# Expert results fetched ahead, three rounds apart, and three contexts moved behind the last expert tile, in a two-layer decoder

## The chip, the cores and the metric

The kernel runs on one core of a Trainium2 chip. The metric is the device time of one execution in microseconds (us). A core has five engines that matter here, each with its own list of instructions that it takes in order: PE (matrix products), DVE (elementwise work and reductions along rows), ACT (functions such as tanh, and copies out of PSUM), POOL (a second, general engine, which here does elementwise products, powers and the indirect transfers) and SP (which only issues transfers). Engines wait for each other by semaphores. On-chip memory is SBUF; matrix products land in PSUM, whose banks are handed round.

## The reference

The input is 32 sequences of 128 tokens with 256 channels. Six blocks follow one another, each added to its input:

```python
x = x + attn(layernorm(x))                 # layer 0: attention over a latent
x = x + xattn(layernorm(x), ctx)           # attention to a context, with distance bias
x = x + ffn(layernorm(x))                  # 2 of 8 experts for each token
x = x + mixer_mlp(x)                       # layer 1: gated linear recurrence, then an MLP
x = x + xattn1(layernorm(x), ctx)          # language-vision attention
x = x + ffn1(layernorm(x))                 # quantised MLP with a convolution over 3 tokens
```

The expert block and the recurrence are what the change touches the neighbourhood of:

```python
weights, top_idx, mask = router(x, Wr, br, top_k=2)
for e in range(8):
    h = relu(x @ W1[e] + b1[e])
    out += (h @ W2[e] + b2[e]) * weights[:, :, e] * mask[:, :, e]

u = k * v                                  # per chunk of 64 tokens
prefix = cumprod(a); acc = cumsum(u / max(prefix, 1e-6))
states = prefix * (state + acc)
y = gate * (q * states) + (1 - gate) * v
```

## The kernel before, in words

The kernel has three phases. `attention()` (until about 655 us) does layer 0's two attentions and the routing weights. `phase_c()` (until about 1221 us) sorts the tokens by expert and runs the experts. `layer1()` does all of layer 1.

**Experts.** Tokens are handled in tiles of 256 tokens of one expert. `brought` loads a tile's weights and gathers its tokens by an indirect transfer on POOL (L807), `tokens` turns them on PE and copies them out (L820), `first_layer` makes h (L832), `second_layer` makes y and adds the bias on DVE (L844), and SP writes the result to the tensor `ys` in HBM (L845). 36 tiles are always needed (`some`); `rest` holds up to a few more, each inside `tc.If(tiles > j)` (L862), where `tiles` is a register that every engine holds. Each engine has a branch at this place.

**Contexts.** Layer 1's language-vision attention needs keys and values of the context, for 16 units of two sequences (T = 256 tokens). `context(u, …)` (L659) returns three pieces: `load` (SP brings the turned context, L666), `keys` (8 matmuls `ck`, then two ACT evictions, L677) and `values` (8 matmuls `cv`, a DVE add, L686, and a write of both to the tensor `ckv` by SP, L690). The first `CTX0 = 6` units are done in `phase_c()` ahead of the expert tiles (L789 to L794), each wholly before the next. The other ten are laid into layer 1's rounds by `CTX_ROUNDS` (L926): for each unit the rounds of its load, keys and values.

**Layer 1.** `unit(u)` (L1043) returns the pieces of one unit of two sequences, 16 units in all. Their order is written by hand: `PLAN` (L910) lists rounds and the names of pieces, and the loop at L1394 walks over rounds t; in a round, it first emits the context pieces filed in `between`, and then, for each unit u, the pieces that PLAN has for round t − STEP·u, with STEP = 11. So a new unit begins every 11 rounds, a unit lasts 90 rounds, and up to nine units are in the air. The instructions of each engine stand in the order in which they are emitted, except that a scheduler may place some POOL instructions; `tc.keep_in_program_order` pins those it is given.

The pieces that the steps below speak of:

- `gather` (L1049): one indirect transfer on POOL (L1054) fetches 128 rows of `ys`, a token's result of one of its two experts, into a tile `yr`, of which there are five buffers. Two sequences times two experts make four per unit. It is pinned in program order.
- `added` (L1060): four DVE instructions (L1063) that add the weighted `yr` to x.
- `d_stats` to `d_flip`: moments on DVE (L967, L968), the inverse root on POOL (`rs_d`, L975; a second one is `rs_d2i` and so on), normalised rows on ACT (L986, L993), the flip on PE (`pt_d`) and its copy `hT_d` on ACT (L1005).
- `d_q`, `d_a`, `d_k`, `d_g`, `d_v`: five products on PE with evictions on ACT; `d_v` also has the product `u_d` on POOL (L1113).
- `d_scan1` (L1136 to L1141), `d_scan2` (L1144, L1145): the recurrence as two scans on DVE; `al_d` is its small copy at L1141. `d_rms` has the product `qn_d` on POOL (L1123).
- `d_state`: a product on DVE (L1148) and a difference `pre_d` on POOL (L1149), which is pinned too. `d_gate` (L1152, L1154) makes `yT_d`.
- `m_y` (L1159) and `m_stats`: x_m on DVE, its inverse root `rs_m` and the sum into x (L1169) on POOL; then the MLP `m_fc`, `m_out`.
- `e_stats`, `e_k`, `e_s`, `e_at` …: the language-vision attention, with the inverse root `rs_e` on POOL.
- `f_h`, `f_z`, `f_taps`, `f_silu`, `f_top` …: the quantised MLP in four quarters; `f_taps` has `z_f` on DVE (L1314) and POOL (L1320), `f_silu` is on ACT (L1327), `f_top` finds the largest absolute values on DVE (`top_f`, L1333).

At layer 1's start, SP loads `we` (L942) and `wc` (L1382), POOL clears the tile `first` (L946), and then the contexts' loads (`cT_k`) and the first fetches follow.

Of the kernel before, what the change touches and what calls it, by code (L numbers as in the profile page):

```python
# [75 lines left out]
def decoder(ctx: ExitStack, tc: tile.TileContext, a: dict, out: bass.AP):  # L76
# [13 lines left out]
    def bank(name, dt=F32):  # L90
        return psp.tile([P, 512 if dt == F32 else 1024], dt, tag="ps", name=name)
# [38 lines left out]
    def vec(name):  # L130
        at, w = PV[name]
        return pv[:, at : at + w]

    def row(name):
        at, w = RV[name]
        return rv[:, at : at + w]
# [68 lines left out]
    def mm(out, lhsT, rhs, start, stop):  # L205
        tc.keep_in_program_order(PE.matmul(out, lhsT=lhsT, rhs=rhs, start=start, stop=stop))  # L206
# [17 lines left out]
    NU = NB // U  # L224
# [434 lines left out]
    def context(u, wcs, turned_tile, kv_tile):  # L659

        wc = wcs.rearrange("p (w c m) -> p w c m", w=2, c=2)
        t = {}

        def load():
            t["cT"] = turned_tile(f"cT_k{u}")
            nc.sync.dma_start(  # L666
                out=t["cT"], in_=a["ctxT"][:, u * T : (u + 1) * T].rearrange("(c p) t -> p c t", p=P)
            )

        def keys():  # L670
            t["kv"] = kv_tile(f"kvc_{u}")
            p = bank(f"ck_{u}").rearrange("p (c t) -> p c t", c=2)
            for c in range(2):
                for k in range(2):
                    mm(p[:, c, :], wc[:, 0, k, c * P : (c + 1) * P], t["cT"][:, k, :], k == 0, k == 1)
            for c in range(2):
                A.activation(  # L677
                    t["kv"][:, 0, c * T : (c + 1) * T], p[:, c, :], AF.Identity, bias=vec("b_lk")[:, c : c + 1]
                )

        def values():
            p = bank(f"cv_{u}").rearrange("p (i d) -> p i d", i=U)
            for i in range(U):
                for c in range(2):
                    mm(p[:, i, :], t["cT"][:, c, i * S : (i + 1) * S], wc[:, 1, c, :], c == 0, c == 1)
            V.tensor_tensor(  # L686
                t["kv"][:, 1].rearrange("p (i d) -> p i d", i=U), p,
                row("b_lv")[:, None, :].to_broadcast([P, U, D]), ALU.add,
            )
            nc.sync.dma_start(out=ckv[u], in_=t["kv"])  # L690

        return load, keys, values

    def load_d():
        w = wpool.tile([P, D_W], F32, tag="w1", name="wd")
        for k in range(2):
            h = D_W // 2
            nc.sync.dma_start(out=w[:, k * h : (k + 1) * h], in_=a["wd"][:, k * h : (k + 1) * h])
        return w


    def phase_c():
        with tc.tile_pool(name="pc", bufs=2) as pool, tc.tile_pool(name="pc1", bufs=1) as keep:
# [82 lines left out]
            V.tensor_scalar(who, pk[:, :NJ], float(NTOK // 2), None, ALU.add)  # L786
            V.tensor_copy(slots, sl)

            for u in range(CTX0):  # L789
                for piece in context(  # L790
                    u, wcs, lambda n: pool.tile([P, 2, T], F32, tag="cT", name=n, bufs=4),
                    lambda n: pool.tile([P, 2, U * D], F32, tag="kv", name=n, bufs=4),
                ):
                    piece()  # L794
            wf = keep.tile([P, 4096], F32, name="wf")

            def brought(j):
# [15 lines left out]
            def tokens(t):  # L813
                j, w, xr = t
                xT = pool.tile([P, 2, TS], F32, tag="xTs", name=f"xTs_{j}")
                pt = bank(f"xs_{j}")
                for h in range(TS // P):
                    for c in range(2):
                        turned(pt[:, c * TS + h * P : c * TS + (h + 1) * P], xr[h][:, c * P : (c + 1) * P])
                V.tensor_copy(xT.rearrange("p c t -> p (c t)"), pt)  # L820
                return j, w, xT

            def first_layer(t):
                j, w, xT = t
                w1 = w[:, : 2 * FF].rearrange("p (c h) -> p c h", c=2)
                b1 = w[:, 2 * FF + NHC * D :]
                hT = pool.tile([P, NHC, TS], F32, tag="hTs", name=f"hTs_{j}")
                for hc in range(NHC):
                    p = bank(f"h_{j}_{hc}")
                    for c in range(2):  # L830
                        mm(p[:, :TS], w1[:, c, hc * P : (hc + 1) * P], xT[:, c, :], c == 0, c == 1)
                    A.activation(hT[:, hc, :], p[:, :TS], AF.Relu, bias=b1[:, hc : hc + 1])  # L832
                return j, w, hT

            def second_layer(t):
                j, w, hT = t
                w2 = w[:, 2 * FF : 2 * FF + NHC * D].rearrange("p (k d) -> p k d", k=NHC)
                b2 = w[:, 2 * FF + NHC * D + NHC :]
                yt = pool.tile([P, TS // P, D], F32, tag="yt", name=f"yt_{j}")
                for h in range(TS // P):  # L840
                    y = bank(f"y_{j}_{h}")
                    for hc in range(NHC):
                        mm(y[:, :D], hT[:, hc, h * P : (h + 1) * P], w2[:, hc, :], hc == 0, hc == NHC - 1)
                    V.tensor_tensor(yt[:, h, :], y[:, :D], b2, ALU.add)  # L844
                nc.sync.dma_start(  # L845
                    out=ys[j * TS : (j + 1) * TS, :].rearrange("(h p) d -> p h d", h=TS // P), in_=yt
                )
# [12 lines left out]
            def rest(j):  # L860
                if j < NT:
                    with tc.If(tiles > j):  # L862
                        second_layer(first_layer(tokens(brought(j))))
                        rest(j + 1)

            t = tokens(brought(0))
            for j in range(some):
                following = brought(j + 1) if j + 1 < some else None
                if j == 1:
                    wd = load_d()  # L870
                    nc.sync.dma_start(out=wf, in_=a["wf"])
                now = first_layer(t)
                t = tokens(following) if following else None
                second_layer(now)
                if j == 3:
                    ternary(wf, keep)
                    for c in range(2):
                        for part, v in (
                            (wd[:, c * 1280 : (c + 1) * 1280], "n1"),
                            (wd[:, 3072 + c * FF : 3072 + (c + 1) * FF], "n2"),  # L880
                        ):
                            A.activation(part, part, AF.Copy, scale=vec(v)[:, c : c + 1])
            rest(some)
        return wd

    def ternary(wf, keep):
# [21 lines left out]

    STEP = 11
    PLAN = (  # L910
        (0, "gather0 gather1"), (1, "gather2 gather3"), (3, "added"), (4, "d_stats"), (5, "d_nb"),
        (6, "d_norm"), (7, "d_scaled"), (8, "d_flip"), (10, "d_q d_a"), (11, "d_k d_g d_scan1"),
        (13, "d_v d_q2"), (14, "d_rms d_scan2"), (15, "d_state"), (16, "d_gate"), (18, "m_y"),
        (19, "m_stats"), (20, "m_scaled"), (22, "m_flip"), (26, "m_fc0 m_fc1"), (27, "m_fc2 m_fc3"),
        (29, "m_out0"), (30, "m_out1 m_out2"), (31, "m_out3"), (32, "e_stats"), (33, "e_nb"),
# [6 lines left out]
    )  # L922


    CTX0 = 6
    CTX_ROUNDS = (  # L926
        (0, 0, 0), (0, 1, 1), (0, 2, 2), (0, 3, 3), (1, 4, 5), (2, 6, 7), (4, 9, 9), (6, 12, 12),
        (9, 14, 15), (12, 16, 17),
    )

    def layer1(wd):
# [8 lines left out]
        with tc.tile_pool(name="pl", bufs=1) as pool, tc.tile_pool(name="pl1", bufs=1) as keep:  # L940
# [442 lines left out]
            between = {}  # L1383
            for u in range(CTX0, NU):
                for piece, r in zip(
                    context(
                        u, wcs, lambda n: sb("d", n, 4), lambda n: sb("kv", n, 2, shape=(2, U * D)),
                    ),
                    CTX_ROUNDS[u - CTX0],
                ):  # L1390
                    between.setdefault(r, []).append(piece)
            units = [unit(u) for u in range(NU)]
            pieces = {r: names.split() for r, names in PLAN}
            for t in range(STEP * (NU - 1) + PLAN[-1][0] + 1):  # L1394
                for piece in between.get(t, ()):
                    piece()
                for u in range(NU):
                    for name in pieces.get(t - STEP * u, ()):
                        units[u][name]()

    attention()
    wd = phase_c()
    routed.close()
    layer1(wd)


# [82 lines left out]
def program(arrays):  # L1489
    import concourse.bacc as bacc  # L1490

    nc = bacc.Bacc("TRN2", target_bir_lowering=False, num_devices=1)
    args = {
        k: nc.dram_tensor(f"in_{k}", v.shape, mybir.dt.from_np(v.dtype), kind="ExternalInput").ap()
        for k, v in arrays.items()
    }
    out = nc.dram_tensor("out", arrays["x"].shape, F32, kind="ExternalOutput").ap()
    with tile.TileContext(nc) as tc:
        decoder(tc, args, out)
    return nc  # L1500
# [9 lines left out]
```

## Time and profile before

| | us |
|---|---|
| median of 5 runs (lowest to highest) | 2036.15 (2033.29 to 2042.11) |
| profiled execution | 2037.04 |
| its span | 2035.3 |
| mean granted PE clock in it | 0.949 |
| busy: PE, DVE, ACT, POOL | 1823.2, 1168.7, 1082.7, 438.0 |
| last expert result written by DVE | 1221.2 |
| first fetch of an expert result, last one | 1224.7, 1827.6 |
| first product of layer 1's contexts | 1232.2 |

The span is the stretch from the first to the last instruction that the hardware profiler saw in one execution; the time of that execution lies a little above it. The granted clock is the share of full speed that PE was given.

In the lines of a profile, L1054 is line 1054 of the kernel. A line of the timeline has start, duration, engine, line, operation, output<-inputs, sizes, and in brackets how long the engine sat idle before it and what ended this. A line of the chain of waits has start, length, and the piece that the end of the kernel waited for at that time, followed back from the last instruction. A line of a group has the count, shortest, median and longest duration in ns, and the first and last start. A line of windows has the stretch, its length, and the busy time of PE, PE's weight loads, DVE, ACT and POOL in it, each with its count of instructions, then the granted clock, the busy share of the DMA engines and GB/s.

### The profile page before, as it was taken

The page shows a single profiled execution, that of the slowest core. Times are in us where ns is not written, and L with a number is a line of the kernel's source. Part 1 is how long each engine was busy: PE and PEld are TensorE (multiplying, and loading weights), DVE is VectorE, ACT ScalarE, POOL GpSimd, SP SyncE. Part 2 cuts the span into 40 slices and gives each one's busy share as a digit, 9 for nine tenths or more (in the row PEclk, how much of TensorE's full clock was granted, in tenths as well). Part 3 has the DMA queues.
Part 4 walks back from the last instruction along what each step waited for, and adds up shares of the span by engine and source line. Part 5 has one row for each costly group of instructions (what it writes and reads, how often), then busy time and mean ns, then how long its engine had stood idle before and what let it go on. Part 6 is the DMA issues. An engine that isn't in the chain of part 4 may idle for free.

```text
span 2035.3 us, 35569 instructions
## 1 busy us (share of the span) xinstructions
PE 1823.2 (90%) x13496; PEld 1496.3 (74%) x13496; DVE 1168.7 (57%) x3716; ACT 1082.7 (53%) x2600; POOL 438.0 (22%) x445
## 2 busy tenths in 40 slices
PE   6999999899987899999999997899998888899863
PEld 4777766677665688888888886678777777777752
DVE  6877667788777512111111013446788778888787
ACT  4454548878785522222222222455666666667662
POOL 4100000000000111111111102333444444443211
PEclk8999999989998799999999998999999999999976
DMA  4000010111002845555555535101011010010000
GB/s 156 3 2 3 7 38 22 33 32 53 12 22 70 293 169 197 183 212 173 210 182 202 196 120 181 52 21 32 22 32 32 27 37 27 27 37 21 27 11 21
DMA packets 53965, 162.65 MB, mean 80 GB/s; under 512 B 5664, under 2 KB 36512, under 8 KB 48672
## 3 DMA queue, kind: packets, MB, share of 16 engines
q1 hardware_dynamic: 47264, 142.52, 19.8%
q0 software_dynamic: 6528, 17.83, 3.1%
q8 instruction: 108, 1.77, 0.3%
q14 instruction: 65, 0.53, 0.1%
HBM read 133.33 MB, written 27.00 MB: 79 GB/s over the span
## 4 chain that ended last, share of the span: by engine, by line
PE 50%; DVE 25%; ACT 10%; POOL 7%; issue 4%; DMA 3%; SPq 0%; POOLq 0%; DVEq 0%; ACTq 0%
PE h L206 12%; PE y L206 12%; ACT sd_b L531 4%; PE od_a L206 3%; DVE top_f L1333 3%; DMA yr<-ys,slots 2%; DVE sd_b L518 2%; PE st_a L206 2%; POOL u_d L1113 1%; POOL z_f L1320 1%; DVE rd_a L497 1%; PE et_b L209 1%; PE ck L206 1%; DVE nm L444 1%; PE q_a L206 1%
## 5 line engine op out<-in xcount | busy, mean ns | idle before, releaser
L832 ACT ACTIVATE hTs<-h,moe 128x256 f32<-128x256 f32 x288 | 136.6, 474 | 374.2 <-PE h L206 374.2
L206 PE MATMUL h<-xTs,moe 128*128 128x256 f32 x1152 | 254.8, 379 | 2.6 <-DVE xTs L820 2.5
L206 PE MATMUL y<-moe,hTs 128*128 128x256 f32 x1152 | 254.6, 379 | 0.0
L206 PEld LDWEIGHTS h<-xTs,moe 128*128 128x128 f32 x1152 | 218.6, 190 | 32.8 <-DVE xTs L820 2.8
L206 PEld LDWEIGHTS y<-moe,hTs 128*128 128x128 f32 x1152 | 216.2, 190 | 27.9
L531 ACT ACTIVATE sd_b<-sd_b,nan_b 128x128 f32<-128x128 f32 x512 | 173.8, 388 | 28.6 <-DVE nan_b L525 28.4
L807 POOL DMA_INDIRECT xr<-xs,who x72 | 68.5, 951 | 437.2 <-PE xs L209 397.9
L820 DVE COPY xTs<-xs 128x512 f32<-128x512 f32 x36 | 24.9, 691 | 234.1 <-PE xs L209 234.1
L844 DVE TENSOR_TENSOR yt<-y,moe 128x256 f32<-128x256 f32 x72 | 30.6, 425 | 215.6 <-PE y L206 215.6
L206 PE MATMUL f_m<-hT_m,wd 128*128 128x256 f32 x512 | 121.1, 391 | 2.6 <-DVE x L1368 2.6
L206 PE MATMUL m_m<-wd,sT_m 128*128 128x256 f32 x512 | 119.8, 382 | 3.5 <-ACT sT_m L1180 3.4
L518 DVE CUSTOM_DVE_ANT_0 sd_b<-nd_b,s_b 128x128 f32<-128x128 f32 x512 | 113.1, 279 | 5.3 <-PE s_b L206 5.3
L206 PEld LDWEIGHTS f_m<-hT_m,wd 128*128 128x128 f32 x512 | 98.0, 197 | 18.0 <-DVE x L1368 4.6
L206 PEld LDWEIGHTS m_m<-wd,sT_m 128*128 128x128 f32 x512 | 95.4, 191 | 16.9 <-ACT sT_m L1180 4.8
L1320 POOL TENSOR_TENSOR z_f<-z_f,e_f 128x508 f32<-128x508 f32 x64 | 70.9, 1107 | 170.8 <-ACT e_f L1318 107.8
L1314 DVE SCALAR_TENSOR_TENSOR z_f<-d_f,pv,z_f 128x254 f32<-128x254 f32 x128 | 64.3, 507 | 58.7 <-ACT z_f L1304 58.3
L1327 ACT ACTIVATE z_f<-z_f 128x512 f32<-128x512 f32 x64 | 40.3, 630 | 104.1 <-POOL z_f L1320 104.0
L497 DVE RECIPROCAL rd_a<-od_a 128x256 f32<-128x256 f32 x32 | 56.0, 1751 | 63.0 <-PE od_a L206 63.0
L544 POOL COPY dens_b<-den_b 128x256 f32<-128x256 f32 x32 | 12.9, 402 | 363.0 <-DVE den_b L542 202.1
L474 ACT ACTIVATE et_a<-st_a 128x512 f32<-128x512 f32 x128 | 66.5, 613 | 27.6 <-PE st_a L206 27.6
L1304 ACT ACTIVATE z_f<-d_f,pv 128x256 f32<-128x256 f32 x128 | 69.6, 590 | 20.6 <-DVE d_f L1299 20.6
L444 DVE TENSOR_REDUCE nm<-s_a 128x4 f32<-128x512 f32 x128 | 79.0, 680 | 2.6 <-PE s_a L206 2.6
(358 smaller groups left out, 4067.8 us busy)
## 6 DMA issues: line engine op xcount, KB each, us to landing
moe<-in_moe SPq DMA_DIRECT2D x36, 2180.0 KB, 9.8
ys<-yt SPq DMA_DIRECT2D x36, 256.0 KB, 2.3
ckv<-kvc SPq DMA_DIRECT2D x16, 512.0 KB, 2.8
kv_e<-ckv SPq DMA_DIRECT2D x16, 512.0 KB, 3.5
x<-in_x SPq DMA_DIRECT2D x8, 512.0 KB, 9.0
cT_b<-in_ctxT SPq DMA_DIRECT2D x8, 512.0 KB, 6.0
xs<-xn_c SPq DMA_DIRECT2D x8, 512.0 KB, 3.0
cT_k<-in_ctxT SPq DMA_DIRECT2D x16, 256.0 KB, 4.7
```

The source lines that it names most:

```text
L206: tc.keep_in_program_order(PE.matmul(out, lhsT=lhsT, rhs=rhs, start=start, stop=stop))
L444: V.tensor_reduce(nms[i % 2][:, at : at + 2 * (P - HD)].rearrange("p (e x) -> p x e", e=2)[:, :2, :], sp[r], AX.X, ALU.max, negate=True,)
L474: A.activation(et[:, r].rearrange("p j q -> p (j q)"), st[r], AF.Exp)
L497: V.reciprocal(rd, od[:, 2 * S :])
L518: V.tensor_tensor_reduce(sd[:, r, j, :], nd[:, i, :], sp[r][:, j, :], SLOPES[head(r, j)], -3e38, ALU.add, ALU.max, mx[:, 4 * r + j : 4 * r ...
L531: A.activation(sd[:, r, j, :], sd[:, r, j, :], AF.Exp, bias=nan[:, 4 * r + j : 4 * r + j + 1], accum_out=den[:, h : h + 1] if r % 2 else None,
L807: GP.indirect_dma_start(out=xr[h], out_offset=None, in_=xs[:, :], in_offset=bass.IndirectOffsetOnAxis(ap=who[:, q : q + 1], axis=0),)
L832: A.activation(hT[:, hc, :], p[:, :TS], AF.Relu, bias=b1[:, hc : hc + 1])
L1304: A.activation(o["z"][:, hc, :], o["d", k][:, j, :], AF.Identity, scale=cw[:, hc, 1:2], bias=cb[:, hc : hc + 1],)
L1314: V.scalar_tensor_tensor(z[:, :, 1:], d[:, j, :].rearrange("p (b t) -> p b t", b=U)[:, :, : S - 1], cw[:, hc, 0:1], z[:, :, 1:], ALU.mult, ...
L1320: GP.tensor_tensor(z[:, :, : S - 1], z[:, :, : S - 1], e.rearrange("p h (b t) -> p (h b) t", b=U)[:, :, 1:], ALU.add,)
L1333: V.tensor_reduce(o["top"][:, k, :], o["z"][:, 4 * k : 4 * k + 4, :].rearrange("p h t -> p t h"), AX.X, ALU.max, apply_absolute_value=True,)
```

## The change

Two things are moved; no operation is added or taken away.

Contexts: those of units 0 to 5 are made as before. Those of units 6, 7 and 8, formerly in layer 1's rounds, are now loaded directly after them in `phase_c()`, and their keys and values stand behind the last of the 36 sure expert tiles, before `rest(some)` with its branches. Seven units, 9 to 15, are left to layer 1's rounds, with rounds of their own.

Fetches: `gather0` to `gather3` and `added` leave PLAN. They are filed in `between`, unit by unit three rounds apart: unit u has them in rounds 3u, 3u + 1 and 3u + 3 in place of 11u, 11u + 1 and 11u + 3, so the last is in round 48 in place of 168. In a round they stand behind the context pieces and ahead of PLAN's pieces of that round. The first piece of PLAN is now `d_stats` in round 4 of its unit. As `gather` and `d_state`'s difference on POOL are both pinned, POOL takes them in the order of the rounds.

```diff
+    CTX_FIRST, CTX0 = 6, 9
...
-            for u in range(CTX0):
-                for piece in context(
+            contexts = [
+                context(
                     u, wcs, lambda n: pool.tile([P, 2, T], F32, tag="cT", name=n, bufs=4),
                     lambda n: pool.tile([P, 2, U * D], F32, tag="kv", name=n, bufs=4),
-                ):
+                )
+                for u in range(CTX0)
+            ]
+            for pieces in contexts[:CTX_FIRST]:
+                for piece in pieces:
                     piece()
+            for pieces in contexts[CTX_FIRST:]:
+                pieces[0]()
...
+            for pieces in contexts[CTX_FIRST:]:
+                for piece in pieces[1:]:
+                    piece()
             rest(some)
...
     PLAN = (
-        (0, "gather0 gather1"), (1, "gather2 gather3"), (3, "added"), (4, "d_stats"), (5, "d_nb"),
-        (6, "d_norm"), (7, "d_scaled"), (8, "d_flip"), (10, "d_q d_a"), (11, "d_k d_g d_scan1"),
+        (4, "d_stats"), (5, "d_nb"), (6, "d_norm"), (7, "d_scaled"), (8, "d_flip"), (10, "d_q d_a"),
+        (11, "d_k d_g d_scan1"),
...
-    CTX0 = 6
+
+    FETCH = ((0, "gather0 gather1"), (1, "gather2 gather3"), (3, "added"))
+    FETCH_STEP = 3
+
     CTX_ROUNDS = (
-        (0, 0, 0), (0, 1, 1), (0, 2, 2), (0, 3, 3), (1, 4, 5), (2, 6, 7), (4, 9, 9), (6, 12, 12),
-        (9, 14, 15), (12, 16, 17),
+        (0, 3, 3), (0, 4, 4), (1, 5, 5), (2, 6, 6), (4, 7, 7), (6, 9, 9), (9, 12, 12),
     )
...
             pieces = {r: names.split() for r, names in PLAN}
+            for u in range(NU):
+                for r, names in FETCH:
+                    for name in names.split():
+                        between.setdefault(FETCH_STEP * u + r, []).append(units[u][name])
             for t in range(STEP * (NU - 1) + PLAN[-1][0] + 1):
```

## The prediction

> **What bounds the kernel now.** I read four views: the page, the chain of waits over one steady period of layer 1, the groups of the fetch, and the timelines of POOL and PE. The page first:
>
> ```profile
> PE 1823.2 (90%) x13496; PEld 1496.3 (74%) x13496; DVE 1168.7 (57%) x3716; ACT 1082.7 (53%) x2600; POOL 438.0 (22%) x445
> PE 50%; DVE 25%; ACT 10%; POOL 7%; issue 4%; DMA 3%; SPq 0%; POOLq 0%; DVEq 0%; ACTq 0%
> ```
>
> PE is busy 90% of the span, but only half of the chain runs through it: layer 1 (from 1222 us on) is a loop through DVE, ACT and POOL in which PE has little slack. One period, in the chain of waits, with pieces left out:
>
> ```profile
> 1779.06 0.84 POOL rs_e L975
> 1779.92 2.87 DMA yr<-ys,slots
> 1782.81 0.48 DVE x L1063
> ...
> 1788.93 1.81 DVE top_f L1333
> ...
> 1792.90 3.50 POOL u_d L1113
> ```
>
> The fetch of an expert result (yr) stands directly behind rs_e. DVE waits 2.87 us for it, does the first of four adds (L1063), and top_f and u_d come after. The same three lines start the next period at 1822.81, so a period is 43.75 us. The group of the fetch:
>
> ```profile
> L1054 POOL DMA_INDIRECT yr<-ys,slots x64: 945/984/1923, 1224.7 to 1827.6; - x64
>   DVE x L1063: 31.2, 34
> DMA to landing us min/median/max: 2.7/3.3/6.2
> ```
>
> All 64 adds together waited 31.2 us for these transfers. Last, the timeline of POOL at six of the sixteen u_d, with the start of layer 1 ahead of them:
>
> ```profile
> 1222.71 0.53 POOL L946 MEMSET first<- 128x512 f32 x1 [63.19 <-SPq L862]
> 1224.73 0.95 POOL L1054 DMA_INDIRECT yr<-ys,slots  x1 [1.50 <-issue]
> 1271.61 1.27 POOL L1113 TENSOR_TENSOR u_d<-u_d,v_d 128x512 f32<-128x512 f32 x1 [22.36 <-ACT v_d L1111]
> 1299.91 1.27 POOL L1113 TENSOR_TENSOR u_d<-u_d,v_d 128x512 f32<-128x512 f32 x1 [1.97 <-ACT v_d L1111]
> 1335.05 1.27 POOL L1113 TENSOR_TENSOR u_d<-u_d,v_d 128x512 f32<-128x512 f32 x1 [0.36 <-ACT v_d L1111]
> 1367.27 1.26 POOL L1113 TENSOR_TENSOR u_d<-u_d,v_d 128x512 f32<-128x512 f32 x1
> 1836.89 3.49 POOL L1113 TENSOR_TENSOR u_d<-u_d,v_d 128x512 f32<-128x512 f32 x1 [6.27 <-ACT v_d L1111]
> 1877.72 2.89 POOL L1113 TENSOR_TENSOR u_d<-u_d,v_d 128x512 f32<-128x512 f32 x1 [8.26 <-ACT v_d L1111]
> ```
>
> The first units follow each other in 28.3, 35.1 and 32.2 us, the last two in 40.83. No fetch lies between those last two (the final one starts at 1827.6), while intervals of u_d with fetches take 43.8. PE at the seam and in the loop:
>
> ```profile
> 1232.21 2.04 PE L206 MATMUL ck<-cT_k,wc 128*128 128x256 f32 x4 [11.45 <-DMA yr<-ys,slots]
> ...
> 1818.69 3.31 PE L206 MATMUL q_d<-hT_d,wd 128*128 128x256 f32 x8 [2.15 <-ACT hT_d L1005]
> 1821.80 2.30 PE L206 MATMUL a_d<-hT_d,wd 128*128 128x256 f32 x8
> ```
>
> PE stands still 11.45 us between the experts and layer 1, and 2.15 us in a period before q_d.
>
> **The change, part by part.** The numbers of fetches (64), adds (64) and contexts (16) stay as they are. Everything is a matter of place.
>
> *Start of the expert stage.* Three keys/values pairs leave it, but the first copy of tokens was held by the contexts and by two long reductions on DVE. It now stands ahead of the reductions. Reading the order by hand, the first h comes some 1.5 us earlier: −1.5. The three loads still issued there put the load of wf behind two context buffers on SP, about 6 us later; tile 0's 14 us hide that.
>
> *The seam.* The three pairs (ck and cv 1.73 us each by issue spacing, 3 × 3.46 = 10.4 us) now follow the last y at 1220.76. They look as if they filled the gap of 11.45 us. But in each engine's list they stand ahead of the branch that closes the sure tiles, and POOL's memset of `first`, the load of `we`, `wc` and the four cT loads on SP and the fetches on POOL come behind it. At present `first` starts 1.50 us after DVE's last yt ends (1221.21). DVE's last new kvc ends near 1220.8 + 10.4 + 0.7 = 1232, so the first fetch moves from 1224.73 to about 1234.3, and layer 1's first ck from 1232.21 to about 1243: +10.5. The gap is moved behind the contexts. Five pairs stand ahead of unit 0's flip in place of six: −3.46. Against that, adds of units 1 and 2 stand between kvc groups on DVE, and q_d of unit 0 needs the bank that such a kvc frees: about +2. Net **+9**. Bounds: +5 if the adds hold nothing, +11 if they hold a whole pair; and below nothing, about −3.5, if the branch does not hold POOL and SP (a rival below).
>
> *The first units (u_d0 to u_d3).* Before, POOL issues 12 fetches in these 95.66 us; after, I count 44 there (20 come earlier, none later). A fetch costs 0.95 + 0.30 us to the next issue, so 32 more are 40 us of POOL. If all fell into POOL's idle time they would cost 0; if all stood on the chain, 40. The windows of this stretch show how much room there is:
>
> ```profile
> 1258.00:1300.00 42.00, 37.55 (x171) 31.15 (x170) 17.29 (x42) 19.14 (x37) 12.30 (x12) 1.00 0.31 111
> ```
>
> POOL (fifth sum) is idle 30 of 42 us, but it takes its list in order. In unit 0, eight fetches stand around pre_d (8 × 1.25 = 10 us), and the eight adds that they feed stand ahead of x_m on DVE; x_m moves from 11.7 us behind u_d0 to 18.7. Four more fetches stand ahead of rs_m, which moves from 16.3 to 25.6. Part of it is caught by slack ahead of u_d1, 28.3 → 34.2 (+5.9). From u_d1 to u_d2, eight fetches precede qn_d (10 us) and PE has that much less of unit 0's work: 35.1 → 39.4 (+4.3). From u_d2 to u_d3, sixteen fetches (20 us) are interleaved: 32.2 → 39.5 (+7.3). That is +17.5; work made ready meanwhile (v_d and its Ln) returns about 2.5 behind it. I take **+15** of the 40, nearer to nothing because most of POOL's row is idle; bounds +8 (two units' delays absorbed) to +25. yr has five buffers; at one fetch in 1.25 us and 2.7 to 3.3 us to land, four are in flight, so buffers bind only where an add is late.
>
> [...] The gather's cost beside DVE first: the copy al_d (L1141) has 155/961/1761 ns as shortest, median and longest, the long ones beside a gather that itself takes 1.69 instead of 0.95. [...] The clock: in 1818 to 1822 the granted clock is 0.65 after a PE wait of 2.15 us, and q_d and a_d spread over 5.25 us between issues instead of 3.46. [...]
>
> *The steady part.* From u_d4 on there are no fetches or adds. From the chain, 2.87 of DMA and four adds of 0.4 to 0.5 leave, and al_d falls from 1.68 (its piece of the same chain) to about 0.16. That is not all gained: z_f of the last quarter (POOL 1.10, then ACT silu) ends only a little earlier and takes their place, so that top_f and u_d come 0.94 us sooner in the half behind rs_e. In the other half, hn_d leaves ACT's queue ahead of e_f0, and z_f, rs_m and hT_d come about 1.9 sooner. Together **2.8 per period**. The row of the last interval, 43.8 − 40.83 = 2.97, says nearly the same without my ordering. Bounds: 0.94 (only the first half) to 4.4 (43.7 − 39.3, PE's own list in a fetch-free stretch, waits for hT_d and at_e removed). Eight full periods (u_d6 to u_d14): 8 × 2.8 = 22.4. Three shorter ones ahead (37.35, 42.6 and 38.6 now): 3 + 4 + 1 = 8, estimated from the fetch's wait and the four adds that leave each. The last period and the 157.6 us behind u_d15 hold no fetch: 0. Sum **−30.4**, bounds −14 to −43.
>
> **Sum.** 2035.3 − 1.5 + 9 + 15 − 30.4 = 2027.4 of span. The profiled run took 2037.04 with a span of 2035.3; the median of the runs, 2036.15, lies 0.85 above that span, so **2028**.
>
> **The rivals.** *POOL's in-order list becomes the bound of the first units* (slower). Its place is rs_m, rs_d and u_d behind fetches between u_d0 and u_d3. For: 44 fetches in a stretch whose chain crosses POOL four times a unit. Against: 30 of 42 us idle. Price: 22 of the 32 additional fetches on the chain, +28, the seam +11, the steady part −20: 2035.3 − 1.5 + 11 + 28 − 20 + 0.85 = 2053.7, about 2053. It decides from where seam and ramp together exceed 38 us. *z_f's last quarter takes the fetch's place* in each period (slower): gain 8 × 0.94 + 8 = 15.5, 2042. For: silu is the next input of top_f. Against: the interval of 40.83. *PE's list is all that is left* (faster): 8 × 4.4 + 8 = 43 with ramp +10: 2010. For: h_f and at_e wait no more in the fetch-free stretch. Against: DVE is 35.66 of 43.76 us busy, and u_d still waits for ACT. *The contexts do fill the gap*, as they would if POOL and SP ran past the branch: seam near 0, 2018. For: 11.45 idle on PE against 10.4 of work. Against: `first` shows 63.19 us idle behind SP's branch before it.
>
> **How the numbers follow.** 0.3% (6.1 us) is about what a measurement can tell from no change. Forecast (own range 2014 to 2041) 0.40: of it 0.22 faster, 0.12 within, 0.06 slower, as 2028 lies only 2 us beyond the bound of 2030. POOL's list 0.22, slower. z_f's place 0.14: 0.10 slower, 0.04 within. PE's list 0.13 and the filled gap 0.11, both faster. Faster 0.46, same 0.16, slower 0.38. The range reaches to PE's list with a shorter ramp (2004) and just beyond POOL's list (2055).
>
> **What would show it.** Seam: the first fetch near 1234 and the first layer-1 ck near 1243, with PE idle about 11 us between; near 1225 and 1232, the rival holds. Ramp: u_d0 near 1280 and u_d3 near 1393 (1367.27 now), POOL nearly full of L1054. Steady: rs_e to rs_e near 41 us from unit 6 on, no yr in the chain, q_d waiting less than 2.15, al_d 0.16 long. I am wrong if u_d0 to u_d3 takes over 125 us, or under 100, or if the period stays above 42.5.

## The result, and the profile after

The changed kernel takes 2040.95 us (median of 30 runs, 2034.37 to 2044.13) where the kernel before takes 2035.82 (57 runs). The ratio is 1.0022, with a 95% interval of 1.0016 to 1.0027: slower, by less than the 0.3% that the prediction set as its limit for no change. The forecast was 2028 us, a gain. The profiled execution has a span of 2038.2 us, 2.9 above that of before.

Cut into stretches by the last expert result on DVE and by POOL's u_d of single units, the two profiled executions compare as follows. Each row is a difference of two starts in the timelines.

| stretch (us) | before | after | difference | forecast |
|---|---|---|---|---|
| start to last expert result | 1220.8 | 1217.9 | −2.9 | −1.5 |
| last expert result to u_d0 (the seam) | 50.8 | 67.9 | +17.0 | +9 |
| u_d0 to u_d3 (the first units) | 95.7 | 123.1 | +27.5 | +17.5 |
| u_d3 to u_d6 | 118.6 | 116.6 | −2.0 | −10.5 |
| u_d6 to u_d14 (eight periods) | 351.0 | 317.8 | −33.2 | −22.4 |
| u_d14 to u_d15 | 40.8 | 38.9 | −1.9 | 0 |
| u_d15 to the end | 157.6 | 156.0 | −1.6 | 0 |
| sum | 2035.3 | 2038.2 | +2.9 | −7.9 |

A loss of 44.5 us in the first 190 us of layer 1 and a gain of 38.7 behind it nearly cancel. The first row is no larger than what the end of the experts varies by among the runs below (1217 to 1223 us). The timeline of POOL in the changed kernel, with `first`, the first fetch and the same six u_d as in the prediction:

```profile
1229.97 0.53 POOL L960 MEMSET first<- 128x512 f32 x1 [73.38 <-DVEq L866]
1233.10 0.95 POOL L1068 DMA_INDIRECT yr<-ys,slots  x1 [2.60 <-issue]
1285.71 1.26 POOL L1127 TENSOR_TENSOR u_d<-u_d,v_d 128x512 f32<-128x512 f32 x1 [20.35 <-ACT v_d L1125]
1321.45 1.26 POOL L1127 TENSOR_TENSOR u_d<-u_d,v_d 128x512 f32<-128x512 f32 x1 [4.51 <-ACT v_d L1125]
1364.46 1.27 POOL L1127 TENSOR_TENSOR u_d<-u_d,v_d 128x512 f32<-128x512 f32 x1 [1.49 <-ACT v_d L1125]
1408.83 1.27 POOL L1127 TENSOR_TENSOR u_d<-u_d,v_d 128x512 f32<-128x512 f32 x1 [3.27 <-ACT v_d L1125]
1843.25 1.28 POOL L1127 TENSOR_TENSOR u_d<-u_d,v_d 128x512 f32<-128x512 f32 x1 [3.73 <-ACT v_d L1125]
1882.17 2.89 POOL L1127 TENSOR_TENSOR u_d<-u_d,v_d 128x512 f32<-128x512 f32 x1 [8.28 <-ACT v_d L1125]
```

`first` is held by DVE's branch at the end of the experts (the releaser in its bracket), as forecast, and the first fetch starts 8.4 us later than before. The first three intervals are 35.7, 43.0 and 44.4 (28.3, 35.1 and 32.2 before).

PE's timeline, first at the seam and then in a steady period:

```profile
1226.28 1.89 PE L206 MATMUL cv<-wc,cT_k 128*128 128x256 f32 x8
1238.40 2.04 PE L206 MATMUL ck<-cT_k,wc 128*128 128x256 f32 x4 [10.23 <-DMA cT_k<-in_ctxT]
...
1270.02 3.78 PE L206 MATMUL q_d<-hT_d,wd 128*128 128x256 f32 x8 [7.99 <-ACT hT_d L1019]
...
1296.70 3.75 PE L206 MATMUL y_m<-wd,yT_d 128*128 128x256 f32 x8 [10.84 <-DVE yT_d L1168]
...
1707.40 1.99 PE L206 MATMUL q_d<-hT_d,wd 128*128 128x256 f32 x8 [0.35 <-ACT hT_d L1019]
1709.23 1.89 PE L206 MATMUL a_d<-hT_d,wd 128*128 128x256 f32 x8
```

The gap of 11.45 us at the seam was not filled: the new pairs run ahead of it, and PE stands still 10.23 us behind the last `cv`. Then there are two long waits, 7.99 us ahead of unit 0's q_d (none before) and 10.84 ahead of its y_m (2.63 before), and the products after them take 3.78 and 3.75 us, twice their usual 1.9. In the steady part the wait before q_d is 0.35 in place of 2.15.

The group of the fetch has all 64 by 1399.3, but DVE waits for them longer than before, 40.7 us in place of 31.2:

```profile
L1068 POOL DMA_INDIRECT yr<-ys,slots x64: 943/957/1487, 1233.1 to 1399.3; - x64
  DVE x L1077: 40.7, 36
```

The chain of waits of a steady period, from rs_e to top_f, no longer has a fetch in it:

```profile
1711.34 0.85 POOL rs_e L989
...
1716.65 0.78 DVE z_f L1328 x2
...
1717.58 1.09 POOL z_f L1334
1718.70 0.64 ACT z_f L1341
1719.36 1.95 DVE top_f L1347
```

top_f starts 8.02 us behind rs_e (9.87 in the lines of before), and what it waits for is z_f's last quarter. The page's busy times hardly changed:

```profile
PE 1823.4 (89%) x13496; PEld 1497.9 (73%) x13496; DVE 1168.0 (57%) x3716; ACT 1083.7 (53%) x2600; POOL 416.7 (20%) x445
```

PE is busy for the same 1823 us. POOL's 21 us less are mostly sixteen u_d (39.8 us, now 26.7) and the fetches (70.6, now 64.2), the same instructions in other company.

### The profile page after: what moved, and what is told of

Its sections match the earlier page's. It is cut to its first block, busy times and chain, and to the rows that moved or that the text cites. A ratio compares the mean times of both kernels' runs of the same rounds, so it can differ in the third digit from the quotient of the medians.

```text
span 2038.2 us, 35586 instructions
## 1 busy us (share of the span) xinstructions
PE 1823.4 (89%) x13496; PEld 1497.9 (73%) x13496; DVE 1168.0 (57%) x3716; ACT 1083.7 (53%) x2600; POOL 416.7 (20%) x445
## 5 line engine op out<-in xcount | busy, mean ns | idle before, releaser
L497 DVE RECIPROCAL rd_a<-od_a 128x256 f32<-128x256 f32 x32 | 56.0, 1751 | 63.1 <-PE od_a L206 63.1
L206 PE MATMUL s_b<-kEO_b,qT_b 32*128 32x256 f32 x512 | 53.2, 434 | 22.9 <-ACT kEO_b L313 17.0
```

Source lines behind the costliest of these rows:

```text
L497: V.reciprocal(rd, od[:, 2 * S :])
```

## The experiments

Twelve kernels were run. Changes shorter than the diff shown in front are given as short diffs. "From the last expert result" means from the start of the last `yt` on DVE; this takes out what the first phases vary by from run to run (that start lies between 1217 and 1223 us).

**Each part alone.** The contexts alone are the changed kernel with the fetches left in PLAN:

```diff
-        (4, "d_stats"), ...
+        (0, "gather0 gather1"), (1, "gather2 gather3"), (3, "added"), (4, "d_stats"), ...
-            for u in range(NU):
-                for r, names in FETCH: ...
```

> Only the contexts are moved; the fetches stay in their places, eleven rounds apart. Theory: the loss of the changed kernel comes from the fetches packed into the first units, so here u_d0 to u_d3 stays near the 95.7 us of before (within 4), the steady period stays at 43.8, the expert stage ends about 2.9 us earlier, the first ck comes near 1238, and the span lies within 6 us of before. Rival: the order of the contexts alone (four pairs in consecutive rounds, with two buffers for their results) makes unit 0 late; then u_d0 comes near 1285 again (1271.6 before) and the span is 2045 or more.

Measured: 2041.25 us, ratio 1.0031 (1.0020 to 1.0042). u_d0 comes 57.8 us from the last expert result (50.8 before, 67.9 in the changed kernel), u_d0 to u_d3 takes 97.0, the period is 43.85. The theory holds for the first units, but the seam is neither what theory nor rival said: the contexts cost 7.0 of its 17.0 us.

The fetches alone are the kernel before with FETCH and FETCH_STEP = 3, and six contexts as before.

> Only the fetches are moved; the contexts stay as before. Theory: u_d0 to u_d3 takes about 123 us as in the changed kernel (95.7 before) and the period falls from 43.8 to about 39.9, a gain of some 38 us behind u_d3; with an unchanged seam the span is about 2025 to 2030. Rival: the moved contexts make the first units slow; then u_d0 to u_d3 is below 108 us and the span near 2010.

Measured: 2035.46 us, ratio 1.0001 (0.9990 to 1.0012). u_d0 comes 61.0 us from the last expert result (+10.2), u_d0 to u_d3 takes 121.6, the period is 39.78. Here too the stretch and the period are as the theory had them, and the span (2033.0) is above its 2025 to 2030 because the seam, which I had taken as unchanged, grew by 10. The two parts add up: 7.0 + 10.2 = 17.2 at the seam against 17.0, and 1.0031 × 1.0001 against 1.0022, which agree within their intervals. What makes the changed kernel slower is the contexts; moving the fetches gains as much as it loses.

**Does the loss go with the number of fetches?**

```diff
-    FETCH_STEP = 3
+    FETCH_STEP = 6
```

> The changed kernel with its fetches six rounds apart in place of three, the last in round 93. Theory: the price of the first units goes with the number of fetches that POOL issues between u_d0 and u_d3 (44 in the changed kernel, some 24 here); then that stretch takes 105 to 112 us in place of 123, the steady period is 39.9 from about unit 9 on, and the span is 2020 to 2030. Rival: the seam and the contexts set the loss; then u_d0 and the stretch stay as in the changed kernel and the span is 2035 to 2045.

Measured: 2024.36 us, ratio 0.9948 (0.9935 to 0.9962). POOL issues 16 fetches between u_d0 and u_d3, not the 24 that I had counted on, and the stretch takes 92.9 us, 30 less than with 44. It does go with the fetches, though not with their number alone: with 16 it is shorter than the 95.7 us of before with 12. Part comes back later (u_d3 to u_d6 takes 126.6, 10 more), and from unit 7 on the period is 39.9.

**The wait for the landing, POOL's issue, the adds.** Here the adds read a constant row, so that the kernel leaves the experts' results out of layer 1:

```diff
-                            x[:, i, :], o.pop(("yr", k)), rw[:, k // U, t : t + 1], x[:, i, :], ALU.mult, ALU.add
+                            x[:, i, :], row("b_lv"), rw[:, k // U, t : t + 1], x[:, i, :], ALU.mult, ALU.add
```

> The changed kernel, but its adds read a constant row in place of the fetched rows; all 64 fetches and 64 adds are still issued in the same order. It leaves the experts' results out of layer 1. It takes away only DVE's wait for the landing (40.7 us before L1077 in the changed kernel). Theory: the first units lose because POOL's in-order list holds 44 fetches between u_d0 and u_d3; then that stretch stays above 112 us (123.1 in the changed kernel) and the span falls by less than 12. Rival: they lose because DVE, with adds ahead of the recurrence in its list, waits for landings; then the stretch comes to 105 or less and the span to 2018 or less.

And without the fetches as well:

```diff
-                for r, names in FETCH:
+                for r, names in FETCH[2:]:
```

> As the run without landings, and the 64 fetches themselves are left out too; the 64 adds stay. It leaves the experts' results out of layer 1. Against the run without landings it takes away POOL's 64 x 1.25 us. Theory: u_d0 to u_d3 falls to 92 us or less, u_d0 to about 1277, and the span to about 2000 or below, as the adds alone are 44 x 0.48 us on a DVE that is half idle. Rival: if the adds are what stands in the way, the stretch stays above 105.

Measured: 2014.26 (ratio 0.9893, 0.9874 to 0.9911) and 1988.74 us (0.9772, 0.9749 to 0.9795). u_d0 to u_d3 takes 108.3 without landings and 82.7 without fetches. The first figure lies between theory (above 112) and rival (105 or less), and the span fell by 25, not by less than 12. These windows, from u_d0 to u_d3 in the changed kernel, the one without landings and the one without fetches, tell more. The columns are the stretch, its length, and busy time with count of PE, PE's weight loads, DVE, ACT and POOL, then the granted clock, the DMA share and GB/s:

```profile
1285.71:1408.83 123.12, 88.16 (x362) 72.12 (x362) 54.92 (x144) 45.75 (x76) 68.17 (x67) 0.85 0.18 53
```

```profile
1278.91:1387.18 108.27, 79.84 (x340) 65.80 (x340) 36.52 (x100) 45.51 (x76) 70.27 (x67) 0.86 0.21 60
```

```profile
1279.91:1362.61 82.70, 71.19 (x332) 60.59 (x332) 34.99 (x100) 45.55 (x76) 23.30 (x23) 0.96 0.03 9
```

POOL has 67 instructions in the first two and 23 in the third: the 44 fetches, and nothing else on POOL, tell the second from the third. With all that goes with them (60 in place of 9 GB/s, a clock of 0.86 in place of 0.96) they cost 25.6 us there. In the chain of waits of the second, the fetches on POOL are the largest part, 33.8% of the stretch. DVE has 144 and then 100: with nothing to wait for, the 44 adds had moved out of layer 1 altogether (their group starts at 414 us), so the first step, 14.8 us, holds the wait and the adds' own time. The expectation had them stay in their places; they did not.

So the adds were pinned to their places, still reading the constant row:

```diff
-                        V.scalar_tensor_tensor(
+                        tc.keep_in_program_order(V.scalar_tensor_tensor(
```

> The changed kernel with adds that read a constant row, as in the run without landings, but pinned to their places on DVE (in the run without landings they had moved far forward, out of layer 1). It leaves the experts' results out of layer 1, and takes away the wait for the landing alone. Of the 14.8 us by which u_d0 to u_d3 fell without landings and adds (123.1 to 108.3), theory: most is the wait, 40.7 us before L1077; then the stretch is 108 to 113 here, and u_d0 comes 57 to 60 us after the last expert result (67.9 in the changed kernel). Rival: it is the 44 adds' own 0.48 us each; then the stretch stays at 118 to 123.

Measured: 2022.95 us, ratio 0.9928 (0.9905 to 0.9952); u_d0 to u_d3 109.0. With 40 of the 44 adds back in the stretch it is hardly longer than without them, so of the 14.8 us about 14 are the wait and under one the adds. At the seam the expectation failed: u_d0 comes 65.5 us from the last expert result, not 57 to 60. The run does not test the wait there, because with pinned adds POOL's list has twelve fetches ahead of unit 1's rs_d where the changed kernel has five, and ACT waits 9.22 us for that root ahead of unit 0's hT_d.

**The seam.** The fetches of units 1 to 15 go nine rounds later, behind the contexts' pieces:

```diff
-                        between.setdefault(FETCH_STEP * u + r, []).append(units[u][name])
+                        between.setdefault(FETCH_STEP * u + r + (9 if u else 0), []).append(units[u][name])
```

> The changed kernel with the fetches and adds of units 1 to 15 nine rounds later, behind the contexts' pieces of rounds 3 to 12. Theory: of the 17.0 us by which u_d0 is late against the last expert result (67.9 in place of 50.8), 10.1 belong to adds that wait for landings ahead of kvc on DVE; then u_d0 comes 57 to 60 us after the last expert result, and as many fetches or more stand between u_d0 and u_d3, so that stretch stays at 118 us or more. Rival: the 17.0 belong to the contexts' own order; then it stays above 64.

Measured: 2040.39 us, ratio 1.0022 (1.0011 to 1.0033). u_d0 comes 58.1 us from the last expert result, as the theory said, and u_d0 to u_d3 takes 125.2. In ACT's timeline of the changed kernel one sees the way in which the adds reached unit 0:

```profile
1257.68 0.81 ACT L677 ACTIVATE kvc<-ck,pv 128x256 f32<-128x256 f32 x2
1261.80 0.84 ACT L677 ACTIVATE kvc<-ck,pv 128x256 f32<-128x256 f32 x2 [3.30 <-DMA ckv<-kvc]
1268.65 0.84 ACT L677 ACTIVATE kvc<-ck,pv 128x256 f32<-128x256 f32 x2 [6.01 <-DMA ckv<-kvc]
1269.38 0.59 ACT L1019 COPY hT_d<-pt_d 128x512 f32<-128x512 f32 x1
```

hT_d, which q_d waits for, stands in ACT's list behind two results kvc. These wait for a buffer of kvc (there are two), the buffer for its write to ckv, the write for DVE's half of the same kvc, and that half for adds ahead of it that wait for landings. On DVE, the last of these adds and that half:

```profile
1263.25 1.10 DVE L1077 SCALAR_TENSOR_TENSOR x<-yr,rw,x 128x256 f32<-128x256 f32 x2 [2.33 <-DMA yr<-ys,slots]
...
1265.00 0.68 DVE L686 TENSOR_TENSOR kvc<-cv,rv 128x512 f32<-128x512 f32 x1
```

In the run with later fetches the waits for ckv are 2.39 and 1.54, and hT_d comes at 1261.29.

**The steady part, with the fetches' order kept.** The kernel before, with adds that read a constant row (they too moved out of layer 1):

> The kernel before with adds that read a constant row; fetches and adds are issued as before. It leaves the experts' results out of layer 1. It takes away the 31.2 us of waits for landings, 2.87 of it on the chain of each period. Theory: that wait, with the work it delays, is most of what a fetch costs in the steady part; then the period is 40 to 41.8 in place of 43.8, and the span 2005 to 2018. Rival: POOL's 5 us ahead of z_f and the collision of al_d with a fetch (1.68 against 0.16) are what costs; then the period stays above 42.5.

Measured: 2012.76 us, ratio 0.9891 (0.9872 to 0.9910), and a period of 41.12: of 43.88 − 39.73 = 4.15 us that the change saves in a period, 2.76 are the wait with the adds, and the other 1.39 what POOL's fetches cost in their old places (with the fetches alone moved, the period was 39.78). With the adds pinned:

> The kernel before with adds that read a constant row and are pinned to their places on DVE; fetches as before. It leaves the experts' results out of layer 1, and takes away the wait for the landing alone. Of the 2.76 us by which the period fell without landings and adds (43.88 to 41.12), theory: the wait is most of it; then the period is 41.1 to 42 and the span 2010 to 2020. Rival: it is the adds' 4 x 0.48 us; then the period is above 42.8.

Measured: 2029.96 us, ratio 0.9971 (0.9956 to 0.9986), period 44.28. The theory's figure fails. The rival's (above 42.8) holds in number only, as the period is longer than before (43.88) though the wait is gone, which the adds' own time can't explain. The chain of waits shows where the pinned adds had come to stand:

```profile
1696.53 1.22 DVE pre_d L1145
1697.75 2.57 DVE x L1063 x4
1700.33 0.07 DVE den_e L1245
```

All four lie on the path between the second scan and at_e. So wait and work of the adds can't be told apart by this run, in which the place of the adds on DVE counts too.

**A version that beats both kernels.** The kernel before, where every unit's fetches are issued five rounds earlier and its adds stay where they are (PLAN is without both, as in the changed kernel):

```diff
+            for u in range(NU):
+                for r, names in ((-5, "gather0 gather1"), (1 - 5, "gather2 gather3"), (3, "added")):
+                    for name in names.split():
+                        between.setdefault(max(STEP * u + r, 0), []).append(units[u][name])
```

> The kernel before, with each unit's four fetches five rounds earlier and its adds in their old place, so that POOL issues them in its idle time ahead of u_d, still one unit at a time. Theory: what a period loses to the fetch is mostly the wait of DVE for the landing and the fetches ahead of z_f; then the wait of L1063 falls from 31.2 us to under 8, the period comes to 40 to 41.5, the first units stay at about 96 us, and the span is 2005 to 2015. Rival: the four adds and POOL's 5 us a unit are what costs; then the period stays above 43 and the span above 2028.

Measured: 2009.34 us, ratio 0.9875 (0.9859 to 0.9891); the profiled execution was a short one, 2002.12. The regular period is 40.2, as the theory said. u_d0 to u_d3 takes 86.0, not about 96, but u_d0 comes 58.0 us from the last expert result in place of 50.8, so that u_d3 is only 2.5 us earlier. The total wait of L1063 did not fall (41.7 us), against the expectation; but all of it lies ahead of 1445 us, in units 0 to 5, the longest 10.0 in the seam, and none behind. The four adds and POOL's 5 us a period then cost 40.23 − 39.88 = 0.35 us together in the regular periods, and 40.38 − 39.73 = 0.65 in the mean of the eight.

Two variants led the fetches from unit 2 or unit 3 on (`ahead = 5 if u >= 2 else 0`, then 3), with the load of wf one tile later:

> The kernel before, each unit's fetches five rounds earlier from unit 2 on (unit 1's in their old place), and the load of the quantised weights one expert tile later. Theory: with unit 1's fetches in their old place, the contexts' results and unit 0's flip come on time again, so u_d0 falls from 1279.6 in the run with all fetches led to 1270 to 1273; the first copy of expert tokens no longer stands behind a reduction, which ends the expert stage 2.6 earlier; the period stays at 40.2 and u_d0 to u_d3 at 86 to 90; the span is 1990 to 1998. Rival: the shorter first units of that run were only the other side of its later u_d0; then u_d3 stays near 1366 and the span near 2000.

> As the run with fetches led from unit 2 on, but led from unit 3 on, so that no adds of unit 2 stand between the contexts' results on DVE. Theory: these adds, which wait for landings ahead of kvc, made u_d0 late; u_d0 then comes 50 to 52 us after the last expert result again (58.0 in the run led from unit 2), u_d3 141 to 146 us after it, the period stays at 40.2 to 41, and the median is 1998 to 2005. Rival: the early units only trade places, and u_d3 stays 147 us or more after the last expert result; then the median stays at 2007 to 2012.

Measured: 2009.24 (0.9876, 0.9853 to 0.9900) and 2008.05 us (0.9871, 0.9850 to 0.9892), neither better than the first to within the intervals. From unit 2 on, the span of 1990 to 1998 was missed, and u_d0 stayed at 58.0 us from the last expert result: four adds of unit 2 stood between the contexts' kvc. From unit 3 on it came at 52.0 and u_d3 at 145.7, both as expected, but u_d3 was no earlier than in the first version (144.0), and with two periods of 43.5 and 42.9, some 6 us over the regular ones, the median stayed above the 1998 to 2005 that were expected. Ahead of the second of them, POOL's timeline of that version has a fetch that takes over 4 us:

```profile
1685.75 0.95 POOL L1055 DMA_INDIRECT yr<-ys,slots  x1 [0.30 <-issue]
1687.00 4.16 POOL L1055 DMA_INDIRECT yr<-ys,slots  x1 [0.30 <-issue]
```

The first version has one such fetch (4.14 us, with a period of 42.9), the two variants have two each. All five stand beside a whole run of seven products z_f and zi_f on DVE and end about 0.8 us behind it; in the other units a fetch at this place takes 1.13 to 1.45 us and stands beside the first three. Why only some units have such a fetch was not tried.

## Why the prediction was wrong, point by point

**The seam, +9.** The contexts' term was right in its total: 10.5 − 3.46 = 7.0 forecast, 7.0 measured with them alone, and the branch held POOL and SP as the prediction said. That the figure fits is partly luck: in that run the first ck came 8.6 us later behind the last expert result, not 10.5, and q_d followed it 1.6 us sooner, not 3.46. The term that failed is "q_d of unit 0 needs the bank that such a kvc frees: about +2". I followed one hop, the bank, and sized it by the adds' own length. The runs showed 10.2, by a longer way: adds wait for landings, hold kvc, which holds the write, the buffer, ACT's next kvc, and hT_d behind it. The bound of +11 for the whole seam was too low as well (17.0). Whether the −1.5 at the start of the expert stage came can't be told from runs that differ by more.

**The first units, +17.5, with 2.5 returned.** The first interval was right: 34.2 forecast, 35.7 measured, with x_m at 19.4 us behind u_d0 (18.7) and rs_m at 26.4 (25.6). The second and third were too short, 39.4 and 39.5 against 43.0 and 44.4. POOL's timeline behind u_d0 shows the mechanism that was named, fetches on both sides of pre_d and ahead of rs_m:

```profile
1291.05 1.44 POOL L1068 DMA_INDIRECT yr<-ys,slots  x1
1292.80 0.95 POOL L1068 DMA_INDIRECT yr<-ys,slots  x1 [0.30 <-issue]
1293.77 1.27 POOL L1163 TENSOR_TENSOR pre_d<-pre_d,v_d 128x512 f32<-128x512 f32 x1
...
1311.09 0.95 POOL L1068 DMA_INDIRECT yr<-ys,slots  x1 [0.31 <-issue]
1312.06 0.73 POOL L989 TENSOR_TENSOR rs_m<-ve_m,mhalf 128x2 f32<-128x2 f32 x1
```

The terms that failed are +4.3 and +7.3 for these two intervals (7.9 and 12.2 measured). They count the fetches on POOL alone and put DVE's wait for the landings at nothing. In the run with pinned adds, which has the fetches but not that wait (and another order of POOL at the seam), the three intervals are 33.5, 40.3 and 35.1, so 2.7 and 9.2 us of the second and third go with the wait, more than the 8.5 us that were missing. The chain of waits agrees: from u_d0 to u_d3 the fetches on POOL are 18.5% of it and the landings 11.2% (8.5% and 8.6% before). I also left out the clock that PE is granted: 0.85 over the stretch against 0.96 before and without fetches, and y_m takes 3.75 us behind waits of 10.84 and 8.67 us and 1.97 behind one of 2.82. What this costs was not measured by itself; the clock is 0.86 in the run without landings too, which is 14.8 us shorter here. The choice of +15 "nearer to nothing because most of POOL's row is idle" was the wrong argument, and +27.5 lies beyond its bound of +25: POOL was idle, but the chain crosses it four times in a unit, and taking out the fetches gave 25.6 us, the landings about 14 more.

**The steady part, −30.4.** Right in kind: −38.7 measured behind u_d3, where −32.9 was forecast (the −30.4 and the 2.5 returned). The eight periods gained 4.15 each, not 2.8, inside the bounds of 0.94 and 4.4. Of the 1.35 that the sum missed, 0.91 lies between rs_e and top_f (1.85 gained, 0.94 forecast). The shorter wait of q_d (0.35 us in place of 2.15) is no part of it: the chain of waits over a steady period has no piece of PE in it, before or after. u_d fell from a median of 3.19 us to 1.28, but this is no gain of its own either, because DVE's zi_f beside it became longer. First before, beside a u_d of 3.49 us, then after, beside one of 1.28:

```profile
1792.98 0.75 DVE L1355 TENSOR_SCALAR zi_f<-z_f 128x512 bf16<-128x512 f32 x2
```

```profile
1683.67 1.82 DVE L1369 TENSOR_SCALAR zi_f<-z_f 128x512 bf16<-128x512 f32 x2
```

Two steady u_d of the changed kernel still take 3.49 us, and the intervals behind them are 40.05 and 40.03 in place of 39.87 or 39.88. The three shorter periods ahead, with the 2.5 to be returned, gained 2.0 and not 10.5; why stays open. As these misses (+8.0 at the seam, +10.0 and +8.5 up to u_d6, −10.8 behind it) have both signs, it is partly luck that the sum is only 10.8 us of span off.

**The rivals.** POOL's list as the bound of the first units came nearest: seam and first units together cost 44.5 us, beyond the 38 from which it was to decide, but the steady part gave more than its 20. The row that spoke against it (30 of 42 us idle) begins 13.6 us ahead of u_d0; from u_d0 to u_d3 POOL was idle 59.9 of 95.66 us. z_f's last quarter did take the fetch's place ahead of top_f, but top_f gained 1.85 us there and not 0.94, and the rest of the period more. (By its own terms that rival comes to 2043 and not 2042, the filled gap to 2019 and not 2018.) The gap was not filled. The period came within 0.25 us of what PE's list as the only bound would give, and PE is 38.21 us busy in a period of 39.90; but with no piece of PE in the chain, that this list is the bound is not shown, and the shorter ramp did not come.

**The clock and the copy al_d.** The prediction has the clock of one period, unit 14's: 0.65 in 1818 to 1822 after a wait of 2.15 us. Not every period shows such a loss. Before the change, a wait of 2.14 to 2.16 us stands ahead of q_d in units 8 to 15. After five of them the clock stays 1.00 and q_d and a_d take 3.56 us; after the last three it is 0.57 to 0.61 over 4 us, and they take 5.17 to 5.24. A period with such a loss is no longer than one without, 43.76 us both:

```profile
1749.14:1792.90 43.76, 38.91 (x204) 32.86 (x203) 35.65 (x92) 29.53 (x58) 20.19 (x18) 0.96 0.10 31
1705.38:1749.14 43.76, 38.45 (x208) 32.40 (x207) 35.75 (x92) 29.54 (x58) 20.20 (x18) 1.00 0.09 31
```

The copy al_d came to 0.16 us as forecast: in the changed kernel it has 160/164/172 ns, and none met a fetch. But a fetch is not the whole of the long copies before. Each of the eight (1751 to 1761 ns) stood 0.59 us beside a fetch and then 1.10 us beside POOL's product z_f (L1320), with whose end it ended, and two short ones (155 and 167 ns) stood wholly beside a fetch. That a fetch alone stretches al_d is not shown.

## What to carry to other kernels

A transfer that stands on the path because its issue comes just ahead of its use was cured here by distance, not by going first: a lead of five rounds, in the engine's idle time, was worth 26 us, and all units' transfers near the start were worth nothing in sum (ratio 1.0001), because the seam and the first units lost what the steady part gained. Where an instruction that waits is moved into another place of an in-order list, follow all that stands behind it to the end, over buffers and writes too; the first hop gave 2 us, the whole way 10. And work laid into a gap fills it only if what ends the gap can start before the work: here PE's 11.45 us became 10.23 behind the moved contexts.

## What the runs showed of the hardware that had not been expected

Waits of PE of the same length were followed by different granted clocks. In the traces of the kernel before and of the changed kernel, from 1220 us on, the granted clock is 1.00 or 0.50, and its changes lie 3.41 us or a multiple of it apart. For rows of 3.41 us laid between these changes, up to 1900 us: sixteen rows at full clock had PE idle for 2.05 us or more, and each was followed by one at half clock; none with 1.96 us or less was. Two waits of 2.15 us ahead of q_d before the change, in two rows each:

```profile
1552.97:1556.38 3.41, 1.45 (x7) 1.30 (x8) 3.41 (x8) 3.12 (x7) 0.89 (x2) 1.00 0.00 0
1556.38:1559.80 3.42, 3.42 (x20) 3.01 (x19) 2.91 (x14) 2.74 (x6) 1.65 (x2) 1.00 0.00 0
...
1815.79:1819.20 3.41, 1.25 (x6) 0.80 (x5) 3.39 (x9) 2.17 (x5) 1.76 (x2) 1.00 0.00 0
1819.20:1822.62 3.42, 3.42 (x9) 2.70 (x9) 3.17 (x13) 2.20 (x6) 0.70 (x1) 0.50 0.01 5
```

The first wait has 1.96 us in its row and 0.19 ahead of it, and the clock stayed 1.00; the second lies wholly in its row, and the clock of the next was 0.50. In the first units of the changed kernel, with waits of 5.6 to 10.8 us ahead of single products, the clock from u_d0 to u_d3 was 0.85.

An indirect fetch took 0.96 us of POOL in the median of the changed kernel (0.98 before), but in the versions with led fetches one or two in each run took 3.96 to 4.16 us, and the period around them was some 3 us longer (42.9 to 44.2 in place of 40.2).
